# Four stacked graph-attention layers on one core: layer 2's token transposes by DMA and VectorE, exp straight from the scores bank, masks by ScalarE

## The chip, the cores and the metric

The kernel runs on one core of a Trainium2 chip. The metric is the device time of one execution in microseconds (us). The core has a matrix engine (TensorE, PE in the profile), three engines for everything else (VectorE is DVE, ScalarE is ACT, GpSimd is POOL), and SyncE (SP), whose queue issues most of the DMAs here. Matrix products land in banks of PSUM, which VectorE and ScalarE empty; all other tiles are in SBUF, 128 partitions high.

## What is computed

128 graphs of 64 nodes with 512 features each pass through four layers. Every layer normalizes its tokens, applies relu, runs an attention over each graph's adjacency, and adds the result to the residual. Layers 0 and 2 are the same kind, with four heads of 64:

```
h = max(layernorm(x), 0)
q, k, v = split_heads(h @ Wq), split_heads(h @ Wk), split_heads(h @ Wv)
sim = (q . k) * 64 ** -0.5
sim = where(adjacency, sim, -float32_max)
x = x + (softmax(sim) . v) @ Wo + bo
```

Layer 1 has eight heads, a second layernorm and a diagonal that is always allowed. Layer 3 is a graph convolution: cosine similarities of mapped tokens are compared with 0.1 and multiplied with an attention. All data are float32.

## The kernel before

**Tiling.** The 8192 tokens are cut into 16 steps of 512 tokens (`TB` = 4 blocks of 128 partitions, two graphs to a block). The program runs over 64 pairs (l, s) of layer and step. A step of layer 0 or 2 goes through these stages: the tokens are loaded into `xin` (line 486), normalized in place (`scales` and `normalize`, lines 443 to 459), turned so that features lie on partitions (`hT`), multiplied with the query-key and value-output weights (`winograd`, whose products are all at line 613; seven products of half-size blocks with sums of blocks made ahead by GpSimd or VectorE), then scores (line 930), softmax, a transpose of the probabilities, the product with v (`po`, line 1097), the output product, the addition to the residual tile `xres`, and a store to DRAM (line 1065) that sets `x_done` for the next layer's load.

**Order.** The order is written out by a planner that runs when the program is built. Every stage is a generator; it yields `(engine, duration, latency)` ahead of each instruction, or an event that it waits for. `Order.run` picks the stream that can start first on its engine, then the one with the lower priority number. The resulting order on each engine and each DMA queue is fixed: an instruction that waits holds up all that stand behind it in its queue. A `Ring` is a set of n buffers given out in turn: the k-th request waits until request k - n has been released. A `Bank` gives out whichever buffer is free.

**How tokens are turned.** `transposes` (line 554) knows two ways. For most steps of layers 1 and 3 `turned_tokens` lets ScalarE (line 534) and, for three blocks, GpSimd move 32 x 128-element pieces between partition groups, and VectorE transposes 32 x 32 blocks (line 544). For all steps of layers 0 and 2, and for two steps of each other layer, TensorE transposes 16 blocks of 128 x 128 (line 570) into PSUM tiles `ptr`, and ScalarE evicts each group of four to `hT` (line 574). After that `has_h` takes a tile of `t` for the sums of blocks, sets `h_ready`, and `sums_of_b` makes the sums on GpSimd (line 366).

**Softmax.** `softmax_parts` (line 934) works on the scores bank `sc`, of which there is one (`r_sc`, also used for `po`). VectorE writes the large negative number where the mask says so (line 941), takes the maximum of each of the 16 rows of 64 (line 947), and subtracts it into the SBUF tile `E` (line 949); then the bank is released (`se.set()`). ScalarE takes the exponential of `E` in place with scale 0.125 (line 952), VectorE sums the rows (line 959), and `divide` multiplies by the reciprocal on GpSimd (line 965). `transposed` moves pieces by ScalarE (line 974) and transposes on VectorE (line 979).

**Masks.** `masks` (line 983) loads the adjacency bytes of a step (line 988) and makes the mask `n0` from them. In layers 0 and 2 this is one VectorE instruction, adjacency equal to zero (line 1005).

**Buffers and streams that the change touches.** `xin` has 2 buffers, `h` 2, `t` 3, `qk` 3 (layers 0 and 2 use one a step, layers 1 and 3 two), `e` 2. The DMAs on SP's queue are the token loads (line 486), masks (988), residual loads (1020, 1135), stores (1065, 1154) and the small ones of layer 3 (881 to 905). The streams are spawned with the priorities 4 for loads and layernorms, 3 for transposes, 5 for projections, 1 for softmax and its transposes, 2 for attention.

Of the kernel before, what the change touches and what calls it, by code (L numbers as in the profile page):

```python
# [8 lines left out]
F32 = mybir.dt.float32  # L9
U8 = mybir.dt.uint8  # L10
AF = mybir.ActivationFunctionType
ALU = mybir.AluOpType
AX = mybir.AxisListType

P = 128
D = 512
N = 64
TB = 4
NC = D // P
# [184 lines left out]
def pe(us):  # L204
    return ("pe", us, 0.25)
# [6 lines left out]
def dve(us):  # L212
    return ("dve", us, 0.1)


def act(us):
    return ("act", us, 0.1)
# [6 lines left out]
def load(us=2.2):  # L224
    return ("sp", 0.6, us)
# [3 lines left out]
def gnn_stack(ctx: ExitStack, tc: tile.TileContext, a: dict, out: bass.AP):  # L229
    nc = tc.nc  # L230
    x_d = a["x"]
    NG = x_d.shape[0] // (P * TB)
    od = Order()

    def ring(tag, n, shape, dtype=F32, space=None):
        kw = {} if space is None else {"space": space}
        p = ctx.enter_context(tc.tile_pool(name=tag, bufs=n, **kw))
        return Ring(od, p, n, shape, dtype, tag)
# [4 lines left out]
    const = ctx.enter_context(tc.tile_pool(name="const", bufs=1))  # L243
# [7 lines left out]
    r_h = ring("h", 2, [P, NC, TB * P])  # L251
    r_t = bank("t", 3, [P, NC, 2, H])
    r_qk = ring("qk", 3, [P, NC, TB * P])
# [15 lines left out]
    x_done = {}  # L269
# [17 lines left out]
    sel = const.tile([P, 32], F32, name="sel")  # L287
    nc.vector.memset(sel, 0.0)

    bdw = const.tile([P, P], F32, name="bdw")  # L290
    nc.vector.memset(bdw, 0.0)
    for g in range(2):
# [163 lines left out]
    def normalize(v, rs, func):  # L456
        for t in range(2):
            yield act(0.81)
            nc.scalar.activation(v[:, t, :], v[:, t, :], func, bias=rs[:, 2, t:t + 1],  # L459
                                 scale=rs[:, 0, t:t + 1])  # L460

    hT, hB, h_ready, h_done, t_done = {}, {}, {}, {}, {}

    def quarters(v):

        return lambda j, k: v[:, 2 * j:2 * j + 2, k * H:(k + 1) * H]

    loaded, l_ready = {}, {}

    def loads(steps):  # L470
        for l, s in steps:
# [22 lines left out]
    normed, n_ready = {}, {}  # L494

    def layernorms(steps, half):

        for l, s in steps:
            yield l_ready[l, s, half]
            whole, xe = loaded.pop((l, s, half))  # L500
            x = whole[:, 2 * half:2 * half + 2, :]
            rs = yield from scales(x)
            yield from normalize(x, rs, AF.Relu)
            if l == 1:
                rs = yield from scales(x)
                yield from normalize(x, rs, AF.Identity)
            normed[l, s] = whole, xe
            n_ready[l, s, half].set()

    def turned_tokens(l, s):  # L510
# [40 lines left out]
        h_ready[l, s].set()  # L551
        return h

    def transposes(steps):

        for l, s in steps:
            if (l, s) in [(1, 2), (1, 3), (1, 4), (1, 5), (1, 6), (1, 7), (1, 8), (1, 9), (1, 10), (1, 11), (1, 12), (1, 13), (1, 14), (1, 15), (3, 2), (3, 3), (3, 4), (3, 5), (3, 6), (3, 7), (3, 8), (3, 9), (3, 10), (3, 11), (3, 12), (3, 13), (3, 14), (3, 15)]:
                h = yield from turned_tokens(l, s)
            else:
                h, h_done[l, s] = yield from r_h.new("hT")  # L560
                hT[l, s] = h
            for half in range(0 if (l, s) in [(1, 2), (1, 3), (1, 4), (1, 5), (1, 6), (1, 7), (1, 8), (1, 9), (1, 10), (1, 11), (1, 12), (1, 13), (1, 14), (1, 15), (3, 2), (3, 3), (3, 4), (3, 5), (3, 6), (3, 7), (3, 8), (3, 9), (3, 10), (3, 11), (3, 12), (3, 13), (3, 14), (3, 15)] else 2):
                yield n_ready[l, s, half]
                x, xe = normed[l, s]
                for t in range(2):
                    b = 2 * half + t
                    pt, pe_ = yield from r_tr.new("ptr")
                    for c in range(NC):
                        yield pe(0.115)
                        nc.tensor.transpose(pt[:, c, :], x[:, b, c * P:(c + 1) * P], ident)  # L570
                    if b == TB - 1:
                        xe.set()
                    yield act(0.6)
                    nc.scalar.copy(h[:, :, b * P:(b + 1) * P], pt)
                    pe_.set()
                if (l, s, half) == (0, 0, 0):
                    yield from has_h(l, s, h)
            if (l, s) != (0, 0) and (l, s) not in [(1, 2), (1, 3), (1, 4), (1, 5), (1, 6), (1, 7), (1, 8), (1, 9), (1, 10), (1, 11), (1, 12), (1, 13), (1, 14), (1, 15), (3, 2), (3, 3), (3, 4), (3, 5), (3, 6), (3, 7), (3, 8), (3, 9), (3, 10), (3, 11), (3, 12), (3, 13), (3, 14), (3, 15)]:
                yield from has_h(l, s, h)
            yield from sums_of_b(quarters(h), hB[l, s][1], (l, s) == (0, 0))  # L580
            hB[l, s][2].set()
            if (l, s) == (0, 0):
                first_t.set()

    def has_h(l, s, h):
        T, t_done[l, s] = yield from r_t.new("T")
        hB[l, s] = (quarters(h), T, od.event())
        h_ready[l, s].set()
# [138 lines left out]
    st, p_ready, s_ready, p_used, o_used, turn = {}, {}, {}, {}, [], []  # L727
# [203 lines left out]
                                         lT[r, c, k], rT[r, c, k], start=True, stop=True)  # L931
        return S, e

    def softmax_parts(S, se, E, mask, neg, masked):

        m = mask.rearrange("p b k -> p (b k)")
        n = m.shape[1]
        sv = S.rearrange("p a (c m) -> p (a c) m", m=n)
        shape = [P, 1024 // n, n]
        yield dve(1.5)  # L940
        nc.vector.copy_predicated(sv, m[:, None, :].to_broadcast(shape),
                                  negs[:, neg:neg + 1, None].to_broadcast(shape))
        masked.set()
        S3 = S.rearrange("p a (i k) -> p (a i) k", k=N)
        mx = soft.tile([P, 16], F32, tag="mx", name="mx")
        yield dve(1.2)
        nc.vector.tensor_reduce(mx, S3, AX.X, ALU.max)
        yield dve(1.2)
        nc.vector.tensor_tensor(E, S3, mx[:, :, None].to_broadcast([P, 16, N]), ALU.subtract)  # L949
        se.set()  # L950
        yield act(1.06)
        nc.scalar.activation(E, E, AF.Exp, scale=0.125)  # L952
        sm = soft.tile([P, 2, 16], F32, tag="sm", name="sm")
        yield from row_sums(sm[:, 0, :], E)
        return sm

    def row_sums(o, E):
        yield dve(1.2)
        nc.vector.tensor_reduce(o, E, AX.X, ALU.add)  # L959
# [23 lines left out]
    def masks(l, s):  # L983

        adj, ae = yield from r_adj.new()
        n = TB * N
        yield load(3.5)
        nc.sync.dma_start(adj.rearrange("p b k -> p (b k)"), a["adj"][:, s * n:(s + 1) * n])
        n0, ne = yield from r_n0.new()
        if l == 3:  # L990
            nz = small.tile([P, TB], U8, tag="nz", name="nz", bufs=1)
            yield dve(0.3)
            nc.vector.tensor_scalar(nz, adj[:, :, 0], 0.0, None, ALU.is_equal)

            yield dve(0.6)
            nc.vector.scalar_tensor_tensor(n0, adj, 0.0, nz[:, :, None].to_broadcast([P, TB, N]),
                                           ALU.is_equal, ALU.mult)
            return adj, ae, n0, ne
        yield dve(0.6)
        if l == 1:  # L1000

            nc.vector.scalar_tensor_tensor(n0, adj, 0.0, noteye[:, None, :].to_broadcast(
                [P, TB, N]), ALU.is_equal, ALU.mult)
        else:
            nc.vector.tensor_scalar(n0, adj, 0.0, None, ALU.is_equal)
        ae.set()
        return n0, ne, None, None
# [182 lines left out]

    def softmax(l, z, u, S, se, m, masked):
        E = z["e", u][0]
        sm = yield from softmax_parts(S, se, E, m, (0, 1, 0, 2)[l], masked)
        z["sm", u] = sm
        if l < 3:
            yield from divide(E, sm[:, 0, :])
            z["e_ready", u].set()
        z["exp", u].set()
# [52 lines left out]
    def fronts(steps):  # L1251
        for l, s in steps:
            yield from front(l, s)
# [18 lines left out]

    steps = [(l, s) for l in range(4) for s in range(NG)]
    for k in steps:
        for e in (p_ready, s_ready, p_used, h_ready, x_done):
            e[k] = od.event()
        for half in range(2):
            l_ready[(*k, half)], n_ready[(*k, half)] = od.event(), od.event()
    with tc.manual_schedule():
        od.spawn(weights(), 4)  # L1280
        od.spawn(loads(steps), 4)
        for half in range(2):
            od.spawn(layernorms(steps, half), 4)
        od.spawn(transposes(steps), 3)
        od.spawn(projections([k for k in steps if k[0] < 3]), 5)
        od.spawn(fronts(steps), 1)
        od.spawn(turns(steps), 1)
        od.spawn(attentions(steps), 2)
        od.run()
# [45 lines left out]
```

## Time and profile before

| | us |
|---|---|
| time, median of 3 runs | 2790.13 (2788.91 to 2795.86) |
| time of the profiled execution | 2791.22 |
| its span | 2789.2 |
| VectorE busy in layer 2 (1290 to 1842 us) | 359.8 |
| ScalarE busy in layer 2 | 339.7 |
| ScalarE busy in layer 0 (14 to 530 us) | 326.4 |
| transposes of tokens on TensorE (line 570) | 576 instructions |
| DMA packets in the span | 160430 |

The span is what the profiler saw of the execution's instructions; the time of the same execution is 2.0 us longer. An engine's busy time is the sum of its instructions' intervals. Matrix products overlap on TensorE, so a record of one is longer than the pace at which they follow each other. In the rows of the profile, `out<-in` names the tiles, a number after `x` is a count, and what stands after the last bar is the idle time of the engine before such instructions and the releaser that ended it.

### The profile page before, as it was taken

The numbers are of one execution on the slowest core, as the hardware profiler recorded it, in microseconds if no ns is written. First come the engines' busy times: TensorE is split into PE (matmuls) and PEld (weight loads), VectorE is DVE, ScalarE is ACT, GpSimd is POOL, SyncE is SP. The second block draws the span as 40 slices with busy tenths as digits, with TensorE's granted clock in tenths as the row PEclk, the third lists the DMA queues.
The fourth block names the chain that finished last, engine by engine and source line by source line (L and its number), as shares of the span: only waits on it lengthen the run. The fifth ranks groups of instructions, "written<-read, shape, count | busy, mean of one in ns | idle before, by whom it ended". The sixth has DMA issues, their size and how long they took to land.

```text
span 2789.2 us, 63654 instructions
## 1 busy us (share of the span) xinstructions
PE 2723.9 (98%) x26728; PEld 2362.1 (85%) x26728; DVE 1896.2 (68%) x2780; ACT 1872.4 (67%) x3149; POOL 1608.2 (58%) x1242
## 2 busy tenths in 40 slices
PE   8999999999999999999999999999999999999997
PEld 7888888888888888888888888878888888888876
DVE  6766767677767667766657666746777667776656
ACT  5756756688777777776656656657566776677644
POOL 5667667645435445446656576676665656555543
PEclk9999999999999999999999999999999999999998
DMA  4333333212112111112322242332422233223221
GB/s 157 108 107 109 108 116 114 96 63 77 47 62 77 47 61 64 61 47 97 122 93 92 93 138 93 108 104 78 111 64 63 71 93 86 64 63 84 73 63 47
DMA packets 160430, 238.51 MB, mean 86 GB/s; under 512 B 23952, under 2 KB 69008, under 8 KB 160144
## 3 DMA queue, kind: packets, MB, share of 16 engines
q1 hardware_dynamic: 145632, 219.98, 25.4%
q10 hardware_dynamic: 14512, 14.47, 1.6%
q8 instruction: 210, 3.44, 0.5%
q14 instruction: 76, 0.62, 0.1%
HBM read 166.77 MB, written 67.63 MB: 84 GB/s over the span
## 4 chain that ended last, share of the span: by engine, by line
PE 91%; DVE 4%; POOL 2%; ACT 1%; issue 1%; DMA 1%; POOLq 0%; SPq 0%; ACTq 0%; DVEq 0%
PE mA L613 46%; PE mC L613 23%; PE mB L613 12%; PE sc L930 5%; PE po L1097 2%; PE ptr L570 2%; PE po L1242 1%; PE mmn L872 1%; POOL xres L1045 1%; POOL xres L1024 1%; ACT F L974 1%; DVE xres L643 1%; DVE E L949 0%; DVE t L363 0%; POOL E L965 0%
## 5 line engine op out<-in xcount | busy, mean ns | idle before, releaser
L974 ACT COPY F<-E 32x512 f32<-32x512 f32 x768 | 472.5, 615 | 41.0 <-POOL E L965 26.3
L1045 POOL TENSOR_TENSOR xres<-xres,u 128x512 f32<-128x512 f32 x192 | 259.9, 1361 | 296.3 <-ACT u L1040 236.1
L1024 POOL TENSOR_TENSOR xres<-xres,u 128x512 f32<-128x512 f32 x192 | 260.8, 1380 | 23.0 <-DMA xres<-x 17.0
L366 POOL TENSOR_TENSOR t<-hT 128x512 f32<-128x512 f32 x126 | 181.4, 1440 | 145.7 <-DVE hT L544 89.0
L459 ACT ACTIVATE xin<-xin,rs 128x512 f32<-128x512 f32 x320 | 247.8, 810 | 19.4 <-DVE rs L452 15.6
L630 ACT COPY v<-mA 128x256 f32<-128x256 f32 (+1 forms) x192 | 92.0, 479 | 218.5 <-PE mA L613 205.5
L534 ACT COPY t<-xin 32x512 f32<-32x512 f32 x364 | 224.1, 616 | 6.4
L450 POOL TENSOR_TENSOR rs<-rs,mhalf 128x2 f32<-128x2 f32 x160 | 115.9, 726 | 192.0 <-DVE rs L448 168.7
L443 DVE BATCH_NORM_STATS2 st<-xin 128x6 f32<-128x512 f32 x320 | 214.9, 672 | 15.8 <-DMA xin<-in_x 7.7
L613 PE MATMUL mA<-w_vo,t 128*128 128x128 f32 (+1 forms) x1152 | 204.5, 312 | 1.1 <-ACT u L1040 1.1
L613 PE MATMUL mA<-t,w_qk 128*128 128x256 f32 x768 | 185.9, 381 | 1.5 <-DVE t L363 1.5
L965 POOL TENSOR_TENSOR E<-E,sm 128x1024 f32<-128x1024 f32 x64 | 127.8, 1997 | 100.6 <-DVE sm L963 87.3
L613 PE MATMUL mA<-t,w_q 128*128 128x256 f32 x744 | 179.2, 383 | 0.0
L613 PEld LDWEIGHTS mA<-w_vo,t 128*128 128x128 f32 x1152 | 166.2, 191 | 14.6 <-ACT u L1040 4.3
L613 PE MATMUL mA<-t,w_k 128*128 128x256 f32 x744 | 177.3, 381 | 0.0
L366 POOL TENSOR_TENSOR t<-hT,t 128x512 f32<-128x512 f32 x126 | 168.3, 1336 | 7.7 <-DVE hT L544 4.2
L959 DVE TENSOR_REDUCE sm<-E 128x16 f32<-128x1024 f32 x128 | 154.9, 1210 | 12.8 <-ACT E L952 12.1
L613 PEld LDWEIGHTS mA<-t,w_qk 128*128 128x128 f32 x768 | 144.4, 192 | 20.3 <-DVE t L363 1.7
L613 PEld LDWEIGHTS mA<-t,w_q 128*128 128x128 f32 x744 | 140.5, 191 | 20.8 <-issue 1.2
L613 PEld LDWEIGHTS mA<-t,w_k 128*128 128x128 f32 x744 | 140.3, 190 | 19.4
L979 DVE STREAM_TRANSPOSE pt<-F 128x1024 f32<-128x1024 f32 x96 | 118.7, 1236 | 49.8 <-ACT F L974 49.6
L1040 ACT COPY u<-mA 128x512 f32<-128x512 f32 x144 | 84.4, 586 | 97.7 <-PE mA L613 88.8
(217 smaller groups left out, 6908.9 us busy)
## 6 DMA issues: line engine op xcount, KB each, us to landing
x<-xres SPq DMA_DIRECT2D x96, 512.0 KB
xin<-x SPq DMA_DIRECT2D x96, 512.0 KB
xres<-x SPq DMA_DIRECT2D x64, 512.0 KB
xres<-in_x SPq DMA_DIRECT2D x32, 512.0 KB
u<-rs SPq DMA_DIRECT2D x128, 128.0 KB
xres<-x SPq DMA_DIRECT2D x64, 256.0 KB
out<-xres SPq DMA_DIRECT2D x64, 256.0 KB
xin<-in_x SPq DMA_DIRECT2D x30, 512.0 KB
```

The source lines that it names most:

```text
L366: nc.gpsimd.tensor_tensor(o, i0, i1, ALU.subtract)
L443: nc.vector.bn_stats(st, v[:, t, :])
L459: nc.scalar.activation(v[:, t, :], v[:, t, :], func, bias=rs[:, 2, t:t + 1], scale=rs[:, 0, t:t + 1])
L534: nc.scalar.copy(o, v)
L613: nc.tensor.matmul(o, l, r, start=(first and m == 0 and k == 0), stop=(k == KC - 1), skip_group_check=True)
L930: nc.tensor.matmul(S[g * N:(g + 1) * N, par, col], lT[r, c, k], rT[r, c, k], start=True, stop=True)
L959: nc.vector.tensor_reduce(o, E, AX.X, ALU.add)
L965: nc.gpsimd.tensor_mul(E, E, sm[:, :, None].to_broadcast([P, 16, N]))
L974: nc.scalar.copy(F[g * N + 32 * k:g * N + 32 * (k + 1), :, 32 * i:32 * (i + 1)], E[g * N + 32 * i:g * N + 32 * (i + 1), :, 32 * k:32 * (k ...
L979: nc.vector.transpose(o, F)
L1024: nc.gpsimd.tensor_add(xr[:, t, :], xr[:, t, :], bo[l])
L1045: nc.gpsimd.tensor_add(v, v, both(u))
```

## The change

Fourteen steps of layer 2 (2 to 15) get a third way of turning tokens. A new stream `moves` waits for both halves to be normalized, takes a buffer `F` of the `qk` ring, and issues 16 DMAs on SP's queue, each of which moves one 32-partition group of `xin` to another partition group of `F`, in pieces of 32 elements. `by_vector` then waits for these DMAs and has VectorE transpose 32 x 32 blocks in two instructions into `hT`. TensorE's 16 transposes and ScalarE's four evictions of each of these steps go. `moves` goes on to its next step only when VectorE has taken the previous `F`.

In layers 0 and 2 the softmax no longer subtracts on VectorE. The maximum is multiplied by -0.125, and ScalarE takes 16 exponentials of 64 columns each straight from the bank, with that as bias; the bank is released after the last of them. The mask of these layers is made by ScalarE as 1 - adjacency.

```diff
@@ const
+    ones = const.tile([P, 1], F32, name="ones")
+    nc.vector.memset(ones, 1.0)
@@ tokens
+    by_dma = [(2, 2), (2, 3), (2, 4), (2, 5), (2, 6), (2, 7), (2, 8), (2, 9), (2, 10), (2, 11), (2, 12), (2, 13), (2, 14), (2, 15)]
+    def moves(steps):
+
+        fe = None
+        for l, s in steps:
+            for half in range(2):
+                yield n_ready[l, s, half]
+            if fe:
+                yield fe
+            x, xe = normed.pop((l, s))
+            F, fe = yield from r_qk.new("F")
+            Fv = F.rearrange("p c n -> p (c n)").rearrange("p (a i f) -> p a i f", i=4, f=32)
+            xv = x.rearrange("p b (c k f) -> p (b c) k f", c=NC, k=4)
+            for k in range(4):
+                for i in range(4):
+                    yield ("sp", 0.7, 4.0)
+                    nc.sync.dma_start(Fv[32 * k:32 * (k + 1), :, i], xv[32 * i:32 * (i + 1), :, k])
+            xe.set()
+            before, fe = fe, od.event()
+            moved[l, s] = F, before, fe
+            f_ready[l, s].set()
+
+    def by_vector(l, s):
+
+        yield f_ready[l, s]
+        F, fe, taken = moved.pop((l, s))
+        h, h_done[l, s] = yield from r_h.new("hT")
+        hT[l, s] = h
+        F = F.rearrange("p c n -> p (c n)").rearrange("p (b c n) -> p b c n", b=TB, c=NC)
+        for b in range(0, TB, 2):
+            yield dve(1.25)
+            nc.vector.transpose(h.rearrange("p c (b n) -> p b c n", b=TB)[:, b:b + 2], F[:, b:b + 2])
+        fe.set()
+        taken.set()
+        return h
+
     def transposes(steps):
 
         for l, s in steps:
...
+            if (l, s) in by_dma:
+                h = yield from by_vector(l, s)
+            elif (l, s) in turned:
                 h = yield from turned_tokens(l, s)
@@ softmax_parts
-        yield dve(1.2)
-        nc.vector.tensor_tensor(E, S3, mx[:, :, None].to_broadcast([P, 16, N]), ALU.subtract)
-        se.set()
-        yield act(1.06)
-        nc.scalar.activation(E, E, AF.Exp, scale=0.125)
+        if narrow:
+            yield dve(0.1)
+            nc.vector.tensor_scalar(mx, mx, -0.125, None, ALU.mult)
+            for i in range(16):
+                yield act(0.21)
+                nc.scalar.activation(E[:, i, :], S3[:, i, :], AF.Exp, bias=mx[:, i:i + 1], scale=0.125)
+            se.set()
+        else:
+            yield dve(1.2)
+            nc.vector.tensor_tensor(E, S3, mx[:, :, None].to_broadcast([P, 16, N]), ALU.subtract)
+            se.set()
+            yield act(1.06)
+            nc.scalar.activation(E, E, AF.Exp, scale=0.125)
@@ masks
+        if l != 1:
+
+            yield act(0.4)
+            nc.scalar.activation(n0, adj, AF.Identity, bias=ones, scale=-1.0)
+            ae.set()
+            return n0, ne, None, None
@@ softmax
-        sm = yield from softmax_parts(S, se, E, m, (0, 1, 0, 2)[l], masked)
+        sm = yield from softmax_parts(S, se, E, m, (0, 1, 0, 2)[l], masked, l in (0, 2))
@@ streams
+        od.spawn(moves(by_dma), 3)
         od.spawn(transposes(steps), 3)
```

More of the change, by code (lines that the diff above doesn't have):

```diff
@@ L466, in quarters @@
         return lambda j, k: v[:, 2 * j:2 * j + 2, k * H:(k + 1) * H]
-    loaded, l_ready = {}, {}
+    loaded, l_ready, moved, f_ready = {}, {}, {}, {}
+    by_dma = [(2, 2), (2, 3), (2, 4), (2, 5), (2, 6), (2, 7), (2, 8), (2, 9), (2, 10), (2, 11), (2, 12), (2, 13), (2, 14), (2, 15)]
+    turned = [(1, 2), (1, 3), (1, 4), (1, 5), (1, 6), (1, 7), (1, 8), (1, 9), (1, 10), (1, 11), (1, 12), (1, 13), (1, 14), (1, 15), (3, 2), (3, 3), (3, 4), (3, 5), (3, 6), (3, 7), (3, 8), (3, 9), (3, 10), (3, 11), (3, 12), (3, 13), (3, 14), (3, 15)]
     def loads(steps):
@@ L552, in turned_tokens @@
         return h
+    def moves(steps):
[29 more added lines that the diff above has]
+        return h
     def transposes(steps):
         for l, s in steps:
-            if (l, s) in [(1, 2), (1, 3), (1, 4), (1, 5), (1, 6), (1, 7), (1, 8), (1, 9), (1, 10), (1, 11), (1, 12), (1, 13), (1, 14), (1, 15), (3, 2), (3, 3), (3, 4), (3, 5), (3, 6), (3, 7), (3, 8), (3, 9), (3, 10), (3, 11), (3, 12), (3, 13), (3, 14), (3, 15)]:
+            if (l, s) in by_dma:
+                h = yield from by_vector(l, s)
+            elif (l, s) in turned:
                 h = yield from turned_tokens(l, s)
@@ L561, in transposes @@
                 hT[l, s] = h
-            for half in range(0 if (l, s) in [(1, 2), (1, 3), (1, 4), (1, 5), (1, 6), (1, 7), (1, 8), (1, 9), (1, 10), (1, 11), (1, 12), (1, 13), (1, 14), (1, 15), (3, 2), (3, 3), (3, 4), (3, 5), (3, 6), (3, 7), (3, 8), (3, 9), (3, 10), (3, 11), (3, 12), (3, 13), (3, 14), (3, 15)] else 2):
+            for half in range(0 if (l, s) in turned + by_dma else 2):
                 yield n_ready[l, s, half]
@@ L577, in transposes @@
                     yield from has_h(l, s, h)
-            if (l, s) != (0, 0) and (l, s) not in [(1, 2), (1, 3), (1, 4), (1, 5), (1, 6), (1, 7), (1, 8), (1, 9), (1, 10), (1, 11), (1, 12), (1, 13), (1, 14), (1, 15), (3, 2), (3, 3), (3, 4), (3, 5), (3, 6), (3, 7), (3, 8), (3, 9), (3, 10), (3, 11), (3, 12), (3, 13), (3, 14), (3, 15)]:
+            if (l, s) != (0, 0) and (l, s) not in turned:
                 yield from has_h(l, s, h)
@@ L932, in scores, with softmax_parts @@
         return S, e
-    def softmax_parts(S, se, E, mask, neg, masked):
+    def softmax_parts(S, se, E, mask, neg, masked, narrow=False):
         m = mask.rearrange("p b k -> p (b k)")
@@ L1274, in gnn_stack @@
     for k in steps:
-        for e in (p_ready, s_ready, p_used, h_ready, x_done):
+        for e in (p_ready, s_ready, p_used, h_ready, f_ready, x_done):
             e[k] = od.event()
```

## The prediction

> **What bounds the kernel now.** I read the page's busy line first, then the busy times by stretch of the span (cut at the layers), then the chain of work that ended last, then the waits of TensorE in layer 2, and last the single rows that price the change.
>
> The busy line, then the four stretches (layer 0, layer 1, layer 2, layer 3; columns are length, busy us of each engine with counts, granted clock, DMA share, GB/s):
>
> ```profile
> PE 2723.9 (98%) x26728; PEld 2362.1 (85%) x26728; DVE 1896.2 (68%) x2780; ACT 1872.4 (67%) x3149; POOL 1608.2 (58%) x1242
> ```
>
> ```profile
> 14.00:530.00 516.00, 503.18 (x4850) 447.29 (x4849) 363.61 (x584) 326.40 (x552) 345.38 (x272) 1.00 0.34 112
> 530.00:1290.00 760.00, 759.70 (x6829) 657.68 (x6828) 525.80 (x785) 593.42 (x918) 368.33 (x307) 1.00 0.19 64
> 1290.00:1842.00 552.00, 537.29 (x5136) 477.60 (x5136) 359.81 (x556) 339.67 (x578) 346.35 (x273) 0.99 0.31 105
> 1842.00:2789.00 947.00, 921.35 (x9909) 777.50 (x9908) 639.32 (x830) 608.27 (x1099) 545.63 (x383) 0.98 0.28 75
> ```
>
> TensorE is idle 65 us of 2789, in every layer the others have a fifth or more to spare. The chain agrees:
>
> ```profile
> PE 91%; DVE 4%; POOL 2%; ACT 1%; issue 1%; DMA 1%; POOLq 0%; SPq 0%; ACTq 0%; DVEq 0%
> ```
>
> Inside a step of layer 2 the chain is TensorE without a break, and the token transposes (line 570) stand in it with 0.44 us for each four (start, length, what):
>
> ```profile
> 1496.82 0.44 PE ptr L570 x4
> 1497.26 1.30 PE mB L613 x6
> 1498.55 0.44 PE ptr L570 x4
> ```
>
> What TensorE waits for in 1260 to 1850 us is little (sum, times, longest):
>
> ```profile
> PE mC L613 <- DVE xres L643: 5.3, 2, 3.5
> PE po L1097 <- DVE pt L979: 3.0, 2, 2.8
> PE po L1097 <- DVE E L949: 2.5, 3, 1.1
> ```
>
> So time here is what TensorE has to issue. Work taken off TensorE counts in full; work moved between the other engines counts only where it makes TensorE wait.
>
> [...] a group of four transposes is recorded as 0.60 us, yet the next begins 0.44 us later. I therefore price transposes by the pace in the chain, not by the record. [...] 471 ns with a bias against 372 without for 256 columns from a bank, and two such in 0.84 us. [...] The trace has only a write and a read of 128-byte rows, priced below. [...]
>
> The rows used, of ScalarE and of VectorE (the mean ns stands after the sum):
>
> ```profile
> L952 ACT ACTIVATE E<-E 128x1024 f32<-128x1024 f32 x96 | 101.5, 1057 | 9.4 <-DVE E L949 8.9
> L574 ACT COPY hT<-ptr 128x512 f32<-128x512 f32 x144 | 84.4, 588 | 14.7 <-PE ptr L570 13.1 <-issue 1.0
> ...
> L630 ACT COPY v<-mA 128x256 f32<-128x256 f32 x96 | 35.7, 372 | 97.8 <-PE mA L613 85.6 <-DVE v L654 8.1 <-PE mB L613 3.9
> ...
> L634 ACT ACTIVATE m<-mA,vecs 128x256 f32<-128x256 f32 x96 | 40.3, 471 | 90.1 <-PE mA L613 90.0
> ```
>
> ```profile
> L949 DVE TENSOR_TENSOR E<-sc,mx 128x1024 f32<-128x1024 f32 x96 | 117.0, 1219 | 1.8
> ...
> L544 DVE STREAM_TRANSPOSE hT<-t 128x1024 f32<-128x1024 f32 x56 | 66.7, 1223 | 12.3 <-ACT t L534 11.9
> ```
>
> **The change part by part.**
>
> *Token transposes, 14 steps of layer 2.* Removed: 14 x 16 = 224 transposes, in 56 groups of four at 0.44 us: 24.6 us of TensorE's path. With them go 56 evictions of 0.588 us, 2.35 us of ScalarE a step. Added: two VectorE transposes a step at 1.22 us, 2.45 us. VectorE has 192 of 552 us free, so this is hidden unless it comes just when hT is wanted.
>
> *The moves.* Sixteen DMAs a step on SP's queue, each 32 partitions x 16 pieces of 128 bytes: 512 pieces, 64 KB. Data: in a stretch where nearly only a 16 KB read of such rows runs,
>
> ```profile
> 1928.40:1929.60 1.20, 1.20 (x7) 1.06 (x6) 1.17 (x2) 0.84 (x2) 0.00 (x0) 1.00 0.09 14
> ```
>
> 0.09 x 1.2 us x 16 engines = 1.7 us for 14 GB/s x 1.2 us = 131 rows: 13 ns each. So 512 x 13 / 16 = 0.42 us a DMA, 6.7 us a step, 0.23 of a 29.4 us step (the query-key products start at 1493.14 and 1551.87, two steps apart) on top of the 0.31 share that is there. Issue:
>
> ```profile
> 1901.65 5.01 SPq L905 DMA_DIRECT2D u<-rs  x8
> 1906.71 2.61 SPq L1135 DMA_DIRECT2D xres<-x  x4
> ```
>
> ```profile
> 1502.53 0.87 SPq L486 DMA_DIRECT2D xin<-x  x2
> ```
>
> 0.63 and 0.65 us in runs of eight and four, 0.44 in pairs; the shortest on line 486 is 0.36, the longest 1.28. I take 0.65: 10.4 us a step; the ends are 5.8 and 20.5. SP's other issues of a step are two loads, a mask, two stores and two residual loads, 7 x 0.45 = 3.1 us, so SP is less than half busy. Queued behind the moves are the stores (which end x_done), residual loads (TensorE's wait on line 643 hangs on these) and masks.
>
> *The loop of the moves.* A move starts when both halves are normalized and VectorE has taken the previous F, so only one F is alive. One turn is 16 x 0.65 = 10.4 to issue, about 3 to land (an estimate from rs<-rn, issued at 1946.35, with the reads that wait for it at 1949.38), 2.45 of transposes, 1.5 of queueing on VectorE and 3.1 of other issues on SP: 20.5 us against a new step of 29.4 - 1.76 = 27.6. Hidden with 7 us in hand. The third qk buffer is spare in layer 2 (one qk tile a step), so F takes no one's place; xin, two buffers, is held some 10 us longer out of two steps of 27.6.
>
> *Exp from the bank, 32 softmaxes in layers 0 and 2.* VectorE loses 1.22 us and gains a 16-column multiply (about 0.15). ScalarE: [...] less the 0.10 overlap that the pair of 0.84 us shows: 0.21, sixteen make 3.4 us against 1.06, so 2.3 more. Bounds 0.11 (bias free) to 0.31 (no overlap): 0.7 to 3.9 more. The scores bank, of which there is one, is given back after the exps instead of after the subtraction: 0.15 + 3.4 - 1.22 = 2.3 us later. Queued behind it is the po product of the previous step, and po feeds ScalarE, the sums and the output product. TensorE has other products to put ahead of it.
>
> *Masks, 32.* 0.55 us off VectorE (line 1005, mean 547 ns), [...].
>
> ScalarE's sum: layer 0 +2.8 us a step, 45 in all, 326 to 371 of 516 us (72%); layer 1 runs at 593 of 760 (78%) with TensorE full. Layer 2: +2.8 - 2.35, level. VectorE: layer 0 minus 1.6 a step, layer 2 plus 0.85. All of it is hidden by TensorE; the cost when the cover fails is the bank's 2.3 us.
>
> **Sum.** Minus 24.6 us, all from the transposes; nothing for the rest. The profiled execution took 2791.22 (span 2789.2 and 2.0 around it), 1.1 above the median of the runs. 2791.2 - 24.6 = 2766.6, and from the median 2790.13 - 24.6 = 2765.5. I say 2766. What is late next is TensorE's own products.
>
> **The rivals.**
>
> A, the forecast: 2766, its own range 2757 to 2775 for stalls that shift by some us either way when the order changes. Chance 0.63.
>
> B: the stalls grow. The transposes were pieces that TensorE could put between dependent products, and the bank is held 2.3 us longer. TensorE already waits 4.9 us in six waits for line 949 over the kernel, against which most steps wait nothing. Were 32 steps to lose 0.4 us each, that is 13 us: 2779. Chance 0.15; a third of it lies within 0.3% of before.
>
> C: the stalls shrink. Layer 0 and 2 hold 12.8 and 14.7 us of idle TensorE, part of it residuals behind VectorE and GpSimd; with VectorE freed in layer 0, 10 to 15 could go: 2753. Against it: most of these waits end on GpSimd or DMA, which get nothing lighter. Chance 0.08.
>
> D, slower: the moves don't keep up. The place is SP's queue with the one-F loop, the price is t for each DMA. The turn is 16t + 10; it is hidden to t = 1.10, breaks even with the old step at 16t + 10 = 29.4, t = 1.21, and is slower beyond. At 1.28, the longest single issue of line 486, a step is 30.5, so 14 x 1.1 = 15 us slower: 2805; at 1.6 it would be 2880. For it: no DMA of this trace has 512 pieces with 128 bytes each between SBUF tiles, and stores that wait on VectorE stand in the same queue. Against it: data of 0.42 and runs at 0.65. Chance 0.14.
>
> **How the numbers follow.** A measurement of this kernel tells about 0.3%, 8.4 us, from no change. Faster: A 0.63, C 0.08, two thirds of B 0.10, together 0.81. Same: 0.05, the rest of B. Slower: D, 0.14. The range 2750 to 2783 takes in A, most of C and of B and leaves out D.
>
> **What would show it.** Line 570's count down from 576 to 352; layer 2 shorter by some 25 us with TensorE's idle near 15; layers 0, 1 and 3 within 5 us of before. Exps of about 0.31 us that start 0.21 apart. Moves 0.6 to 0.8 us apart on SP, and F landed before VectorE wants it. Wrong would be: layer 2 steps of 29 us or more with TensorE waiting for VectorE's hT transpose or its sums (D), or waits of po and scores on ScalarE's exps in both layers (B).

## The result, and the profile after

The changed kernel took 2761.19 us (median of 4 runs, 2757.64 to 2762.88) against 2791.27 for the kernel before (4 runs, 2788.91 to 2795.86): ratio 0.9886, 95% interval 0.987 to 0.9902. That is 30.1 us less; 24.6 had been forecast, and the time lies in the forecast's range. The profiled execution took 2760.36 with a span of 2758.6, 30.6 less in span.

The busy line of the changed kernel, then its busy times in the same stretches as before (the last now ends at 2758):

```profile
PE 2696.9 (98%) x26504; PEld 2339.8 (85%) x26504; DVE 1915.3 (69%) x2777; ACT 1927.5 (70%) x3605; POOL 1609.3 (58%) x1242
```

```profile
14.00:530.00 516.00, 508.00 (x4865) 452.04 (x4864) 376.66 (x574) 371.77 (x812) 351.05 (x274) 1.00 0.34 116
530.00:1290.00 760.00, 757.70 (x6878) 654.99 (x6877) 519.30 (x780) 592.71 (x916) 359.46 (x302) 1.00 0.18 61
1290.00:1842.00 552.00, 539.38 (x5048) 480.19 (x5047) 388.90 (x591) 361.52 (x796) 374.68 (x295) 1.00 0.51 138
1842.00:2758.00 916.00, 889.10 (x9709) 750.25 (x9708) 622.82 (x804) 596.04 (x1076) 521.62 (x364) 0.99 0.29 74
```

TensorE has 224 instructions and 27.0 us of busy time less. Its idle time, span minus busy, went from 65.3 to 61.7. Not all of the 27.0 us is work that has gone: in short stretches the clock that TensorE was granted is 0.50 (the last section shows one, in which eight products, nearly all of their time at 0.50, took 3.50 us against 1.99 at 1.00), so that half of its busy time there is lost. By the clock records of the two traces that loss is 11.7 us before and 6.5 after (half of 23.4 and 13.0 us of TensorE's busy time). So the 30.6 us are 21.8 of work, 5.2 of half clock and 3.6 of idle time. ScalarE in layer 0 rose from 326 to 372 us, near the forecast's 371 (in which 0.5 us a step for the mask was the author's estimate; the 32 masks took 0.52 in the mean, line 1051), and nothing came of it; the DMA share of layer 2 went from 0.31 to 0.51 (0.54 computed). Two landmarks place the gain: the first product with layer 1's value weights, and the last with layer 2's. Rows of the two tiles before (count, durations, first and last start):

```profile
L613 PE MATMUL mA<-w_v,hT x128: 379/379/483, 516.4 to 1327.6; 128*128 128x256 f32 x128
```

```profile
L613 PE MATMUL mA<-w_vo,t x1152: 272/275/483, 36.5 to 1877.5; 128*128 128x128 f32 x128, 128*128 128x256 f32 x64
```

and after:

```profile
L654 PE MATMUL mA<-w_v,hT x128: 379/379/483, 513.4 to 1325.1; 128*128 128x256 f32 x128
```

```profile
L654 PE MATMUL mA<-w_vo,t x1152: 272/275/483, 36.3 to 1846.5; 128*128 128x128 f32 x127, 128*128 128x256 f32 x65
```

Up to the first landmark 3.0 us are gained, between the two 28.0 (1361.1 to 1333.1), and from there to the end nothing (911.7 to 912.1). Layer 1 gave none of the 28.0, as its last value product of this kind lies only 2.5 us earlier (1327.6 to 1325.1). So layer 2 gave more than its transposes, and layer 0, where TensorE's instructions are the same, gave something too. The waits of TensorE in layer 2 after (1260 to 1850 us) are others than before:

```profile
PE mC L654 <- ACT v L671: 4.3, 1, 4.3
PE mB L654 <- DVE xres L684: 2.7, 1, 2.7
PE mmf L432 <- DVE u L428: 1.6, 1, 1.6
```

ScalarE's added instructions cost what had been forecast. The exponentials in one softmax (start, length, what, count):

```profile
1523.84 2.98 ACT L994 ACTIVATE E<-sc,mx 128x64 f32<-128x64 f32 x14
1526.81 0.59 ACT L671 COPY qk<-mA 128x512 f32<-128x512 f32 x1
1527.29 0.32 ACT L994 ACTIVATE E<-sc,mx 128x64 f32<-128x64 f32 x1
```

A single one takes 0.32 and fourteen take 2.98, so they start (2.98 - 0.32) / 13 = 0.205 us apart; 0.31 and 0.21 had been forecast. An estimate of the 0.31 from rows that the forecast shows: (588 - 372) / 256 = 0.84 ns a column from a bank, so 471 - 192 x 0.84 = 310 ns for 64 columns. An eviction went in between two of them. The moves on SP (shortest, median, longest in ns):

```profile
L573 SPq DMA_DIRECT2D F<-xin x224: 585/630/1427, 1312.6 to 1737.7; - x112
```

0.63 against 0.65; VectorE waited for F only twice in the layer, 3.6 us in all.

VectorE's added multiply of the maximum did not cost the 0.15 us of the forecast, but 0.73 in the mean (167 to 1302 ns). Two of them, and a GpSimd instruction that runs beside the second:

```profile
1522.75 0.17 DVE L991 TENSOR_SCALAR mx<-mx 128x16 f32<-128x16 f32 x1
62.41 0.98 DVE L991 TENSOR_SCALAR mx<-mx 128x16 f32<-128x16 f32 x1
62.10 1.27 POOL L368 TENSOR_TENSOR t<-hT 128x512 f32<-128x512 f32 x1
```

The second multiply ends when GpSimd's instruction does (63.39 and 63.37). So it is in the 26 of 32 that took 0.29 us or more: each ends 0.03 to 0.04 us after a GpSimd instruction. The other six took 0.17 to 0.18. So VectorE gained only 1.22 - 0.73 = 0.5 us a softmax, and with other instructions longer too (the 18 writes of the large negative number in 14 to 530 us took 2.00 us in the mean, 1.62 before) its busy time in layer 0 did not fall by the forecast's 1.6 us a step: it rose, from 363.6 to 376.7 us.

### The profile page after: what moved, and what is told of

Same layout as the page of the kernel before. It is cut to its first block, busy times and chain, and to the rows that moved or that the text cites. A ratio compares the mean times of both kernels' runs of the same rounds, so it can differ in the third digit from the quotient of the medians.

```text
span 2758.6 us, 63992 instructions
## 1 busy us (share of the span) xinstructions
PE 2696.9 (98%) x26504; PEld 2339.8 (85%) x26504; DVE 1915.3 (69%) x2777; ACT 1927.5 (70%) x3605; POOL 1609.3 (58%) x1242
## 3 DMA queue, kind: packets, MB, share of 16 engines
q8 instruction: 208, 3.41, 0.5%
## 4 chain that ended last, share of the span: by engine, by line
PE 93%; DVE 3%; ACT 2%; POOL 1%; issue 1%; DMA 0%; SPq 0%; POOLq 0%; ACTq 0%; DVEq 0%
PE mA L654 47%; PE mC L654 23%; PE mB L654 12%; PE sc L971 5%; PE po L1152 2%; PE ptr L611 1%; PE po L1297 1%; ACT F L1023 1%; PE mmn L913 1%; ACT E L994 1%; DVE mx L988 0%; ACT u L1095 0%; DMA xin<-in_x 0%; POOL t L368 0%; POOL v L886 0%
## 5 line engine op out<-in xcount | busy, mean ns | idle before, releaser
L368 POOL TENSOR_TENSOR t<-hT,t 128x512 f32<-128x512 f32 x126 | 174.9, 1388 | 9.9 <-DVE hT L548 4.2
```

What stands on the lines that cost most here:

```text
L368: nc.gpsimd.tensor_tensor(o, i0, i1, ALU.subtract)
```

## The experiments

The theory was the forecast's: the time is what TensorE has to issue. Three rivals stood against it once 30 us had been measured: VectorE's relief had ended stalls of TensorE; the small pieces of ScalarE had let evictions pass; or the order that the planner wrote had by chance become a better one. Times are medians; the ratio is to the kernel before, run beside.

**The parts alone.** The first run takes back the softmax and the masks, the second the token moves:

```diff
-        sm = yield from softmax_parts(S, se, E, m, (0, 1, 0, 2)[l], masked, l in (0, 2))
+        sm = yield from softmax_parts(S, se, E, m, (0, 1, 0, 2)[l], masked)
-        if l != 1:
...
-            return n0, ne, None, None
```

> Layer 2's tokens by DMA and VectorE, but softmax and masks as before. Theory (what TensorE has to issue): 24.6 us less than before, ratio 0.991, layer 2 shorter by about 25 and layer 0 as before. Rival (the exp from the bank and the masks bring a good part): no more than 20 us less, 0.993 or above. Rival (the rest is the written order's luck): anything between 20 and 32 less.

```diff
-    by_dma = [(2, 2), (2, 3), (2, 4), (2, 5), (2, 6), (2, 7), (2, 8), (2, 9), (2, 10), (2, 11), (2, 12), (2, 13), (2, 14), (2, 15)]
+    by_dma = []
```

> Exp from the bank and masks by ScalarE in layers 0 and 2, all token transposes of layers 0 and 2 on TensorE as before. Theory: nothing to be seen, within 4 us of before, ratio 0.9985 to 1.0015. Rival (relief of VectorE gave the 5.5 us that were not forecast): 5 us less, 0.998, idle time of TensorE down in layers 0 and 2. Rival (longer hold of the scores bank): more than 4 us slower.

> The changed kernel itself, beside the others on the same chip: ratio 0.989 in every theory. If the parts add up, it is the sum of the two parts run alone.

Measured: moves alone 2770.32, ratio 0.9925 (0.9912 to 0.9939), 21.1 us less than the 2791.42 before; exp and masks alone 2776.28, 0.9945 (0.9933 to 0.9958), 15.1 less; both 2759.65, 0.9885 (0.9869 to 0.9901), 31.8 less. The moves are as forecast in TensorE's busy time, which fell from 2723.9 to

```profile
PE 2699.8 (97%) x26504; PEld 2343.3 (85%) x26504; DVE 1923.3 (69%) x2809; ACT 1842.5 (67%) x3093; POOL 1607.1 (58%) x1242
```

which is 24.1 us for the 224 transposes, with the same 11.7 us lost at half clock as before; 4.0 of it came back as idle time (2769.1 - 2699.8 = 69.3). The second run contradicts the forecast: softmax and masks, which take nothing from TensorE, gave 15 us. Its busy line, and its waits of TensorE in 1260 to 1850 us, complete:

```profile
PE 2721.7 (98%) x26728; PEld 2364.4 (85%) x26728; DVE 1903.6 (69%) x2749; ACT 1954.4 (70%) x3661; POOL 1612.4 (58%) x1242
```

```profile
PE mA L654 <- ACT u L1095: 4.4, 10, 0.4
PE po L1152 <- ACT E L994: 1.0, 1, 1.0
PE mA L654 <- ACT m L675: 0.3, 1, 0.3
```

None of the waits for the residual adds (line 643 of before) is left, nor those for `pt` and for the end of the subtraction. Of the 13.5 us by which this run's span is shorter (2789.2 to 2775.7), TensorE's idle time gives 11.3 (65.3 to 54.0) and half clock 5.2 (11.7 to 6.5); the rest of its busy time is 3.0 longer. 36.2 for the parts against 31.8 for both: the gains don't quite add up.

**Is it VectorE's relief?** Four runs without the moves: the exp alone; the masks alone; the exp with VectorE's subtraction kept; and the kernel before with nothing but a number of the planner changed (it stands for the masks of layers 0, 1 and 2 alike, not of layers 0 and 2 only).

```diff
+            yield dve(1.2)
+            nc.vector.tensor_tensor(E, S3, mx[:, :, None].to_broadcast([P, 16, N]), ALU.subtract)
             yield dve(0.1)
             nc.vector.tensor_scalar(mx, mx, -0.125, None, ALU.mult)
@@ in another kernel, masks() of before
-        yield dve(0.6)
+        yield dve(0.3)
```

> Of the whole change only the exp from the bank in layers 0 and 2; masks on VectorE and all token transposes on TensorE as before. Exp and masks together gave 15 us. Theory (VectorE relief ends the stalls of TensorE on the residual adds): about 10 us less, ratio 0.9965, since the subtraction is two thirds of VectorE's relief. Rival (the planned order's luck): no relation to the 10; anything from 5 slower to 15 less. Rival (small ScalarE pieces let evictions pass): the full 13 to 15 less.

> Only the masks of layers 0 and 2 by ScalarE. VectorE relief: 3 to 5 us less, ratio 0.9985. Order's luck: anything from 5 slower to 15 less. Small ScalarE pieces: nothing, within 2 us.

> As the run with the exp alone, but VectorE also keeps its subtraction of 1.22 us (its result is overwritten by the exp from the bank), so VectorE is not relieved and the bank is held 3.6 us longer than before. VectorE relief: nothing left of the gain, ratio 0.999 to 1.003. Order's luck: anything. Small ScalarE pieces: the same gain as the exp alone.

> The kernel before with the same instructions; only the duration that the planner assumes for the mask of layers 0 and 2 is 0.3 instead of 0.6 us, so that the written order shifts. VectorE relief and small pieces: within 3 us of before, ratio 0.999 to 1.001. Order's luck: 5 to 15 us away from before, to either side, with other stalls on the residual adds.

Measured beside a before of 2790.2: exp alone 2784.12, 0.9978 (0.997 to 0.9987); masks alone 2792.41, 1.0004 (0.9996 to 1.0013); exp with subtraction 2793.71, 1.0015 (1.0009 to 1.0022); nudged plan 2801.53, 1.0041 (1.0028 to 1.0054). The exp alone and the exp with the subtraction lie 9.6 us apart, as relief would have it. But the masks alone, from which relief promised 3 to 5 us, made no difference clear of noise. The last run has the same instructions as before and is 11.3 us slower, and the two parts of the softmax change make 6.1 - 2.2 = 3.9 us alone and 15.1 together. Nor was VectorE less busy where time was gained: 1896.2 us before, 1909.4 with the exp alone, 1903.6 with exp and masks, 1919.5 with the subtraction kept. And TensorE's waits for residual adds, 12.7 us over the whole kernel before, shrink without relief too: to 3.8 with the subtraction kept and 7.5 in the nudged plan (none with the exp alone). So the written order is worth as much as the effect in question, and these runs can't give the 15 us to VectorE's relief. Against small pieces on ScalarE as the cause speaks that with the subtraction kept they gained nothing, though one order of each is no proof. A bank held 3.6 us longer than before, by the expectation's estimate, was no trouble either: no wait of `po` for the exps was over 0.9 us in that run.

**The transposes of layer 0 too.** Steps 2 to 15 of layer 0 are moved as well, once with the planner's numbers as in the changed kernel, twice with others; and the changed kernel itself with another number:

```diff
+    by_dma = [(l, s) for l in (0, 2) for s in range(2, 16)]
@@ moves, in two other kernels
-                    yield ("sp", 0.7, 4.0)
+                    yield ("sp", 0.67, 2.5)
```

> The changed kernel with steps 2 to 15 of layer 0 also turned by DMA and VectorE: 224 more transposes leave TensorE. Theory: another 24.6 us less, 2761 - 25 = 2736, ratio to before 0.980, and layer 0 shorter by that. Rival (TensorE's transposes filled holes that something else left): well below 25, with TensorE's idle in layer 0 above 13 us.

> The changed kernel with the same instructions; the planner assumes 0.67 and 2.5 us for a move instead of 0.7 and 4.0. If the time is what TensorE has to issue: within 3 us of the changed kernel, ratio 0.988 to 0.9895. If the written order's luck is worth as much as in the nudged kernel of before: 5 to 12 us to either side, with other stalls.

> Layer 0's tokens by DMA too, with the planner's nudge. Theory (the second set of transposes did leave TensorE, and the gain was lost to stalls of another order): the stall of 10.8 us is gone or elsewhere, the time between 2740 and 2757, ratio 0.981 to 0.987. Rival (layer 0's transposes cost nothing, since they stood in holes): 2760 or more again.

> Layers 0 and 2 by DMA, and the planner assumes what the traces show of a move, 0.67 us to issue and 3.5 us to land (2.5 before this, 4.0 in the changed kernel). If a truer plan is what helps: at or below the 2752 of the run with 2.5, ratio 0.983 to 0.987. If the order is luck: anything from 2740 to 2770.

| instructions | planner's latency of a move, us | time | ratio |
|---|---|---|---|
| layer 2 moved (the changed kernel) | 4.0 | 2759.65 | 0.9885 (0.9869 to 0.9901) |
| the same | 2.5 | 2786.03 | 0.9987 (0.998 to 0.9993) |
| layers 0 and 2 moved | 4.0 | 2764.74 | 0.9901 (0.9885 to 0.9917) |
| the same | 2.5 | 2751.79 | 0.9863 (0.985 to 0.9877) |
| the same | 3.5 | 2776.31 | 0.9946 (0.9932 to 0.996) |

Without a changed planner number, moving layer 0 too gained nothing: 2764.74, where 2736 had been expected. Yet layer 0's transposes do leave TensorE's busy time; with the latency of 2.5:

```profile
PE 2682.3 (97%) x26280; PEld 2322.5 (84%) x26280; DVE 1926.1 (70%) x2805; ACT 1896.5 (69%) x3549; POOL 1609.6 (58%) x1242
```

against 2696.9 in the changed kernel: 14.6 of the 24.6 counted, at a lower mean clock (0.991 against 0.995). Half clock costs this run 14.8 us against 6.5, so 22.9 of the 24.6 did go as work. How much of that arrives is a matter of the order. In the first of the three the chain of waits ends in one long stall (start, length, what):

```profile
1605.72 3.00 DMA x<-xres
1608.72 2.37 DVE hT L588 x2
1611.09 0.02 issue
1611.11 0.02 POOLq L368
1611.13 0.09 issue
1611.22 1.26 POOL t L368
```

VectorE's transposes of F start at 1608.72, behind moves that were issued up to 1605.6 (the profile puts the end of their wait to the store issued next, which they don't read); GpSimd's sums follow, then its residual adds, VectorE's add on line 684 at 1618.50, and TensorE after 10.76 us of waiting. In SP's queue the moves of one step stood ahead of a store and of the residual load that these adds want:

```profile
1591.75 13.86 SPq L573 DMA_DIRECT2D F<-xin  x16
1605.72 1.06 SPq L1120 DMA_DIRECT2D x<-xres  x2
1607.21 1.77 SPq L490 DMA_DIRECT2D xin<-x  x2
1609.04 0.54 SPq L1075 DMA_DIRECT2D xres<-x  x1
```

In the changed kernel with latency 2.5 the planner put VectorE's transposes too early: VectorE, whose queue is in order, waited 13.1 us for F (3.6 before), and TensorE stood 7.8 us at one residual add. With layer 0 moved too, the same 2.5 is the best of the three, and VectorE waited 0.6 us for F in layer 2. No latency is right for both; a plan nearer the truth (F was there about 3 us after the last issue had ended, 1605.6 to 1608.7 above) isn't better: 2776.31 is outside both expectations. So is the 26 us that the changed kernel lost with 2.5, more than luck had been given. The kernel at 2751.79 is the fastest of all, by its ratio some 6 us below the changed one, though the intervals of the two just overlap.

**The slower rival.** Each move is cut in two, so that SP has 32 issues a step:

```diff
-                    yield ("sp", 0.7, 4.0)
-                    nc.sync.dma_start(Fv[32 * k:32 * (k + 1), :, i], xv[32 * i:32 * (i + 1), :, k])
+                    for a in range(0, 16, 8):
+                        yield ("sp", 0.7, 4.0)
+                        nc.sync.dma_start(Fv[32 * k:32 * (k + 1), a:a + 8, i],
+                                          xv[32 * i:32 * (i + 1), a:a + 8, k])
```

> The changed kernel with each move cut in two, 32 DMAs a step of 256 pieces each. If each issue costs 0.63 us whatever its size, a turn of the loop is 32 x 0.63 + 10 = 30 us against steps of 27.6: the slower rival's mechanism, 14 x 2.6 = 36 us over the changed kernel, about 2797, ratio 1.002. If the issue goes with the number of pieces (0.36), the turn is 21.5 and the time stays within 10 us of 2761, ratio 0.986 to 0.993.

Measured 2832.73, ratio 1.0156 (1.0142 to 1.017), 72 us over the changed kernel. The issue is 0.609 us for half the pieces, against 0.630 in the changed kernel, so it goes by the DMA and hardly by the size. From 1579.92 on eight steps, 33 to 34 us apart, hold the same stall, two of them here (a step of the changed kernel, between query-key products starting at 1519.64 and 1546.20, has 26.6):

```profile
1646.40 2.04 PE L656 MATMUL mA<-t,w_qk 128*128 128x256 f32 x4 [3.88 <-ACT qk L673]
1680.54 2.04 PE L656 MATMUL mA<-t,w_qk 128*128 128x256 f32 x4 [3.88 <-ACT qk L673]
```

The residual loads stand behind the moves in SP's queue, and GpSimd waited long for them in 1540 to 1840 us:

```profile
POOL xres L1081 <- DMA xres<-x: 65.6, 15, 7.0
```

In the eight steps, though, this is not what holds the time. After its wait for a load GpSimd waits again, for ScalarE's eviction of an output product (`u`), so an earlier load would have gained nothing there:

```profile
1654.96 2.94 POOL L1081 TENSOR_TENSOR xres<-xres,u 128x512 f32<-128x512 f32 x2 [6.91 <-DMA xres<-x]
1663.84 1.26 POOL L1102 TENSOR_TENSOR xres<-xres,u 128x512 f32<-128x512 f32 x1 [5.94 <-ACT u L1097]
```

The chain that ended last is a loop in each of these steps: TensorE, that eviction, GpSimd's second residual adds, its sums and the division of the softmax, ScalarE's moves of the probabilities, its eviction of `qk`, and TensorE again. No DMA is in it. Only earlier in the layer, in parts of 1440 to 1561 us, does the chain pass through the moves and residual loads in SP's queue. The planner, which had 32 issues a step to place, had also written another order for TensorE than in the changed kernel. So most of the 72 us, some 7.5 in each of the eight steps, are lost in that loop of in-order queues; how much a late SP queue would cost with the order kept isn't shown. VectorE's transposes never waited for F in this run: the loop of the single F, which the rival had as its place, wasn't late. The sign and the price of an issue were as the rival said; the place was another.

## Why the prediction was right or wrong

- *24.6 us from the transposes.* Right: 24.1 of TensorE's busy time in the run with the moves alone, 21.1 in time.
- *The moves: issue 0.65, data hidden, F in time.* Right in size, 0.63, and the DMA share was met. Not at nothing, though: moves alone gave back 4.0 us as idle time.
- *Exp and masks on ScalarE, hidden; the bank 2.3 us later, hidden.* Right for ScalarE: exps 0.205 us apart, the mask 0.52 us, and the waits of `po` for exps are 1.9 us in two over the whole changed kernel. Wrong for VectorE: the multiply took 0.73 us in the mean and not 0.15, as 26 of 32 end with a GpSimd instruction, so the bank comes about 2.9 us later (an estimate, 0.73 + 3.4 - 1.22), and the 1.6 us a step that VectorE was to save in layer 0 did not show. No wait of TensorE in the changed kernel names either beyond those 1.9 us.
- *"Nothing for the rest" in the sum.* This step failed. Softmax and masks alone brought 15.1 us. With the moves' 21.1 that is 36.2, and 31.8 were kept. The forecast had it as its rival C, at 0.08, as 10 to 15 us. What the runs show is that with softmax and masks alone TensorE is idle 11.3 us less, with no wait for residual adds left (12.7 us before, 2.7 in the changed kernel), and loses 5.2 us less at half clock. That VectorE's relief is the reason isn't shown: its busy time did not fall, and a nudge of the planner alone moves 11 us and more.
- *The range of A, 2757 to 2775 "for stalls that shift by some us".* Too narrow as a statement on such changes: the same instructions in other orders gave 2760 and 2786, and for layers 0 and 2 moved, 2752, 2765 and 2776. That the changed kernel fell 5 us from the point was partly luck.
- *Idle of 12.8 and 14.7 us in layers 0 and 2.* The sum has no term for the clock. One stall of 1.81 us was followed by half clock that cost 1.7 us more (below), and half clock cost 11.7 us in the kernel before.

## What to carry to other kernels

Count what the bound engine no longer has to issue, at its pace in the chain: in the run with the moves alone that was right to half a microsecond of busy time. Then ask what the written order is worth, by a run with the same instructions and one planner number changed; until that spread is known (here 11 to 26 us), a difference of its size can't be put down to the edit. By that measure the 30 us in time are this order's as much as the edit's; what the edit itself shows is the busy time. Sixteen small DMAs a step cost 0.63 us of SP's queue each; where a residual load stood behind them and F came late, TensorE stood 10.76 us. And a long wait of one engine is a cause only if the chain passes through it: GpSimd's waits of 65.6 us for residual loads were, in the eight steps, followed by waits for something else.

## What was not expected of the hardware

A stall of TensorE may be followed by 3.41 us at half clock. In the kernel before, two stalls of 1.81 us stand before the same eight products, the first in layer 0, the second in layer 2:

```profile
195.53 1.99 PE L613 MATMUL mC<-t,w_qk 128*128 128x256 f32 x8 [1.81 <-DVE xres L643]
1626.85 3.50 PE L613 MATMUL mC<-t,w_qk 128*128 128x256 f32 x8 [1.81 <-DVE xres L643]
```

Two stretches of 3.41 us for each, the one with the stall and the next (the second number is TensorE's busy time, the clock is the third from the end):

```profile
193.57:196.98 3.41, 1.60 (x9) 1.29 (x8) 1.35 (x2) 1.50 (x2) 3.41 (x3) 1.00 0.02 5
196.98:200.39 3.41, 3.41 (x19) 3.01 (x18) 1.42 (x3) 2.17 (x4) 0.23 (x1) 1.00 0.00 0
1623.76:1627.17 3.41, 1.60 (x54) 1.27 (x47) 0.69 (x1) 2.00 (x4) 3.33 (x3) 1.00 0.03 7
1627.17:1630.58 3.41, 3.41 (x10) 2.69 (x9) 1.59 (x2) 0.63 (x2) 1.34 (x2) 0.50 0.00 0
```

The one in layer 2 cost 3.41 x 0.5 = 1.7 us on top of its 1.81, and that time is counted as busy. In the traces of both kernels, ahead of the last stretch (before, half clock from 2770.63 to the end), half clock comes only in pieces of 3.41 us and one of 6.83, twice that; those of the kernel before start at 1446.26, 1627.17, 1835.38, 1992.39 and 2661.41, which is 53, 61, 46 and 196 pieces apart. What sets them isn't shown. The piece of layer 2 followed a stretch with 1.60 us of work; the stretch with the stall of layer 0 held 1.60 us as well and was not followed by half clock. Its 9 products were mostly those of 256 columns, most of the other's 54 the 64 x 64 ones of `po`; whether that made the difference isn't shown.

In the run with split moves a step of 34.1 us at a clock of 0.90 loses 3.4 us this way beside 4.1 us of idle time, together the 7.5 by which it is longer than the step of 26.6.
